# Softmax of three wide-head attentions: one exp for each head and sequence, with the maximum as its bias and the sum as its second result

## The chip, the cores and the metric

The kernel runs on one core of a Trainium2 chip. Its time is device microseconds of one execution; the figure compared is the median of several runs. A separate execution was recorded by the hardware profiler, and all durations of single instructions come from that one. The core's engines are TensorE (PE in the profile; its weight loads are PEld), VectorE (DVE), ScalarE (ACT), GpSimd (POOL) and SyncE (SP), which issues most DMAs. Each engine runs its own instructions in the order in which they were written, and waits on semaphores for the others.

## What is computed

The reference is a decoder of four layers on 32 sequences of 64 tokens of width 256, all in float32. Each layer adds an attention (or a state-space mixer), a cross attention to a context of 64 tokens of width 128, and a feed-forward part. The three attentions of the change are the wide ones:

- **L0_attn**: 32 heads of 64, 8 heads of keys and values, rotary positions, causal: `softmax((q k^T) / sqrt(64))`.
- **L0_xattn**: 16 heads of 128, a mask over the context; where a sequence's mask is empty the output is 0: `softmax(masked(q k^T) / sqrt(128))`.
- **L1_xattn**: 16 heads of 128 with q and k normalised by their root mean square: `softmax((q_n k_n^T) / sqrt(128))`.

```python
scores = jnp.einsum('bhqd,bhkd->bhqk', q, k) / jnp.sqrt(jnp.float32(HD))
scores = jnp.where(causal[None, None], scores, jnp.finfo(scores.dtype).min)
probs = jax.nn.softmax(scores, axis=-1)
o = jnp.einsum('bhqk,bhkd->bhqd', probs, v)
```

## The kernel before

The 2048 tokens are 16 tiles of 128 tokens, so a tile is two whole sequences. Every tile's residual stays on the chip (`X[i]`). The tiles run in three groups of 8, 6 and 2. A group runs its wide stages (L0_attn, L0_xattn, L0_ffn, L1_attn, L1_xattn) while the group before it runs the later, narrow ones, the two streams interleaved by `weave`. The first group runs its first stages alone: L0_attn and L0_xattn of 8 tiles, then L0_ffn and L1_attn, then L1_xattn. A tile has four wide softmaxes: two in L0_attn (16 heads each; `unit_L0_attn`'s loop over `u`), one in L0_xattn and one in L1_xattn. That makes 64 in all.

One softmax works on a tile `s` of 128 partitions x 16 x 64: for each query on its partition, 16 groups of 64 scores, which is one head of one sequence each. TensorE writes the scores to PSUM, and VectorE moves them to `s`, adding the mask or multiplying by the normaliser. Then come five steps on `s`: `shift` takes the maximum of each group (VectorE) and subtracts it from the 1024 columns (`combine`: VectorE or GpSimd); ScalarE takes the exp of all 1024 columns in one instruction, with the attention's scale; `weigh` adds up each group and takes the reciprocal (VectorE); another `combine` multiplies. L0_xattn multiplies the 16 reciprocals by `some`, which is 0 for an empty mask. Then `turn` transposes `s` on TensorE, eight blocks of 128x128, and the products with the values and the output weights follow (`cross_out` in the cross attentions).

Nothing is issued in the order of this code. A `Recorder` collects every operation with the tiles that it reads and writes, and `Order` writes down one fixed order for each engine: it keeps a clock for each engine, prices each operation with `duration`, and again and again takes the operation that can start first, the oldest one where several can. Work may be taken up to 120 us of TensorE work ahead of the oldest open operation, as long as buffers are free: 8 PSUM banks (`mm`), 10 wide tiles (`b4`), 35 small ones (`sm`) and others. An operation of `either` or `combine` may go to two engines, and the planner picks the one that ends it earlier by its prices. In the profile every instruction has line 2340, where the planned order is issued; the instructions are told apart by the names of their tiles, which come from the function that asked for them (`shift_sm`, `weigh_sm`, `L_xattn_b`, `turn_mm`). The prices that the prediction uses are these:

```python
        if method.startswith("reduce") and views[1].dims[-1][0] > 1:
            return 0.15 + n * 0.0017
        return 0.15 + n * 0.00104 + 0.06 * small
    if engine == "scalar":
        if method == "activation":
            return (0.17 if psum else 0.205) + n * 0.00083 + 0.18 * (small and psum)
...
    return 0.14 + n * (0.00174 if full < 2 else 0.0022)
EARLY = {"vector": 0.082, "scalar": 0.1, "gpsimd": 0.04}
```

Here `n` is the number of columns, the last return is GpSimd's, and `EARLY` is how long before the end of an operation the engine takes its next one in the plan.

Of the kernel before, what the change touches and what calls it, by code (L numbers as in the profile page):

```python
# [21 lines left out]
AF = mybir.ActivationFunctionType  # L22
# [18 lines left out]
def _constants():  # L41

    f = np.float32
    r = np.arange(P)
    c = {}
    c["ident"] = np.eye(P, dtype=f)
    c["ones"] = np.ones((P, P), f)

    c["causal"] = np.where(np.arange(64)[None, :] <= (r % 64)[:, None], 0.0, NEG).astype(f)

    c["upto"] = ((r % 64)[:, None] <= np.arange(64)[None, :]).astype(f)

    c["after"] = ((r[:, None] > r[None, :]) & (r[:, None] // 64 == r[None, :] // 64)).astype(f)

    c["before"] = (r[:, None] < r[None, :]).astype(f)

    c["strip8"] = ((r[:, None] % 32) // 8 == np.arange(4)[None, :]).astype(f)
    c["strip16"] = ((r[:, None] % 32) // 16 == np.arange(2)[None, :]).astype(f)

    c["parity"] = (r[:, None] // 64 == np.arange(2)[None, :]).astype(f)  # L60

    c["unit"] = np.broadcast_to(np.eye(1, 32, dtype=f), (P, 32))
    c["iota"] = np.broadcast_to(np.arange(64, dtype=f), (P, 64))
    main = ((r % 64) < 48).astype(f)
    c["mainT"] = np.zeros((P, P), f)
    c["mainT"][0], c["mainT"][1] = main, 1 - main
    c["row"] = r[:, None].astype(f)

    at = (np.arange(NT)[:, None, None] * P + r[None, :, None]) * 6 + np.arange(6)[None, None, :] - NONE
    c["parts"] = np.transpose(at, (1, 0, 2)).reshape(P, NT * 6).astype(f)  # L70
    c["mhalf"] = np.full((P, 32), -0.5, f)

    inv = f(1.0) / f(500000.0) ** (np.arange(0, 64, 2, dtype=f) / f(64))
    ang = inv[r % 32][:, None] * np.arange(64, dtype=f)[None, :]
    co, si = np.cos(ang).astype(f), np.sin(ang).astype(f)
    c["rope0"] = np.concatenate([co, si, si, co], 1)
    inv = f(1.0) / f(10000.0) ** (np.arange(0, 8, 2, dtype=f) / f(8))
    ang = (r % 64).astype(f)[:, None] * inv[None, :]
    co, si = np.cos(ang).astype(f), np.sin(ang).astype(f)
    c["rope3"] = np.concatenate([co, co, -si, si], 1)  # L80
    at, parts, n = {}, [], 0
    for k, v in c.items():
        at[k] = (n, n + v.shape[1])
        n += v.shape[1]
        parts.append(v.astype(f))
    return np.ascontiguousarray(np.concatenate(parts, 1)), at
# [113 lines left out]
def bc(ap, axis, n):  # L200

    u = ap.unsqueeze(axis)
    s = list(u.shape)
    s[axis] = n
    return u.broadcast_to(s)
# [11 lines left out]
def split(ap, a, pat="p (a b) -> p a b"):  # L217
    return ap.rearrange(pat, a=a)
# [157 lines left out]
class Recorder:  # L376
# [7 lines left out]
    def add(self, ways, args, kw, group=None):  # L384

        op = Op()
        op.at, op.ways, op.args, op.kw, op.group, op.behind = len(self.ops), ways, args, kw, group, []
        out = kw["out"] if "out" in kw else args[0]
        op.outs = [out] if isinstance(out, (View, Far)) else []
        views = [v.view if isinstance(v, Rows) else v for v in [*args, *kw.values()]]  # L390
        op.ins = [v for v in views if isinstance(v, (View, Far)) and v is not out]
        op.after, op.tiles, before = [], set(), {}
        for views, write in ((op.ins, False), (op.outs, True)):
            for v in views:
                t, m = v.t, v.mask()
                lo, hi = v.p0, v.p0 + v.n
                if t.psum:
                    lo, hi = 0, P
                op.tiles.add(t)
                for kept in (t.writes, t.reads) if write else (t.writes,):  # L400
                    covered = False
                    for o, l2, h2, m2 in kept:
                        if o is not op and m & m2 and lo < h2 and l2 < hi and (group is None or o.group != group):
                            before[o.at] = True
                            covered = covered or (write and not (m2 & ~m) and lo <= l2 and h2 <= hi)
                    if covered:
                        same = lambda a: group is not None and a[0].group == group
                        kept[:] = [a for a in kept if a[3] & ~m or a[1] < lo or a[2] > hi or same(a)]
        for views, write in ((op.ins, False), (op.outs, True)):
            for v in views:  # L410
                lo, hi = (0, P) if v.t.psum else (v.p0, v.p0 + v.n)
                (v.t.writes if write else v.t.reads).append((op, lo, hi, v.mask()))
        op.waits, op.ready = len(before), 0.0
        for i in before:
            self.ops[i].after.append(op)
            if self.ops[i].group is not None:
                op.behind.append(self.ops[i])
        for t in op.tiles:
            t.left += 1
            if t.first is None:  # L420
                t.first = op.at
            t.last = op.at
        self.ops.append(op)
# [234 lines left out]
class Net:  # L658
# [163 lines left out]
            self.nc.vector.scalar_tensor_tensor(x, ps, rs, x, ALU.mult, ALU.add)  # L822


    def weigh(self, s, sums_of):

        n = s.shape[1]
        sm, r = self.sm(n), self.sm(n)
        self.nc.vector.reduce_sum(sm, sums_of, AX.X)
        self.nc.vector.reciprocal(r, sm)  # L830
        return r

    def shift(self, out, s):

        n, m = s.shape[1], s.shape[2]
        mx = self.sm(n)
        self.nc.vector.reduce_max(mx, s, AX.X)
        self.nc.combine(out, s, bc(mx, 2, m), ALU.subtract)

    def turn(self, p, n):  # L840

# [24 lines left out]
    def unit_L0_attn(self, layer, W, i):  # L866
# [53 lines left out]
        for u in range(2):  # L920

            s = self.b4(16, 64)
            for j in range(2):
                nc.vector.tensor_tensor(
                    s[:, 8 * j : 8 * j + 8], split(sc[2 * u + j], 8), bc(self.k("causal"), 1, 8), ALU.add
                )
            self.shift(s, s)
            nc.scalar.activation(s, s, AF.Exp, scale=0.125)
            r = self.weigh(s, s)
            nc.combine(s, s, bc(r, 2, 64), ALU.mult)  # L930
            ss.append(s)
        terms = []
        for u in range(2):
# [118 lines left out]
    def unit_L0_xattn(self, layer, W, i):  # L1052
        nc = self.nc
        wq, wo = W
        hT = self.norm(layer, [i])
        cx, cT, mu = self.context(i), self.contextT(i), self.tile("cx", P, dtype=U8)
        nc.sync.dma_start(out=mu, in_=self.ins["mask"][i * P : (i + 1) * P].partition_broadcast(P))

        qs = []
        for a in range(2):  # L1060
            q = self.b4(8, P)
            for j in range(0, 8, 4):
                ps = split(self.mm(), 4)
                for u in range(4):
                    self.prod(ps[:, u, :], [(wq[a][:, j + u, c * P : (c + 1) * P], hT[:, c, :]) for c in range(2)])
                self.evac(q[:, j : j + 4, :], ps)
            qs.append(q)
        mf, add, some = self.tmp(P), self.tmp(P), self.sm(2)
        nc.vector.tensor_copy(mf, mu)
        nc.vector.tensor_scalar(add, mf, 1.0, -NEG, ALU.subtract, ALU.mult)  # L1070
        nc.vector.reduce_max(some, split(mf, 2), AX.X)
        ps = self.cross_scores(qs, lambda h, b: cT[:, b * 64 : b * 64 + 64])
        s = self.b4(16, 64)
        for j in range(2):
            nc.vector.tensor_tensor(
                s[:, 8 * j : 8 * j + 8].rearrange("p (a b) n -> p a (b n)", b=2), split(ps[j], 4), bc(add, 1, 4), ALU.add
            )
        self.shift(s, s)
        nc.scalar.activation(s, s, AF.Exp, scale=128.0**-0.5)
        r = self.weigh(s, s)  # L1080

        nc.vector.tensor_tensor(split(r, 8), split(r, 8), bc(some, 1, 8), ALU.mult)
        nc.combine(s, s, bc(r, 2, 64), ALU.mult)
        self.cross_out(i, s, cx, wo, "x0_")


# [278 lines left out]
    def unit_L1_xattn(self, layer, W, i):  # L1365
# [58 lines left out]
        for b in range(4):  # L1424
            self.transpose(pt[:, b, :], rows[:, b * P : (b + 1) * P])
        ve, rq = self.sm(4, 2, 2), self.sm(4, 2, 2)
        nc.vector.tensor_scalar(
            ve, pt.rearrange("p (a b) (m r) -> p m a b r", a=2, r=32)[:, :, :, :, 0], 1.0 / 128, 1e-5, ALU.mult, ALU.add
        )
        self.power(rq.rearrange("p a b c -> p (a b c)"), ve.rearrange("p a b c -> p (a b c)"))  # L1430
        ps = self.cross_scores(qs, lambda h, b: kTs[h // 8][:, h % 8, b * 64 : b * 64 + 64])
# [2 lines left out]
        for j in range(2):  # L1434
            at = slice(8 * j, 8 * j + 8)
            nc.vector.tensor_tensor(s[:, at], split(ps[j], 8), bc(rq[:, at], 2, 64), ALU.mult)
        self.shift(s, s)
        nc.scalar.activation(s, s, AF.Exp, scale=128.0**-0.5)
        r = self.weigh(s, s)
        nc.combine(s, s, bc(r, 2, 64), ALU.mult)  # L1440
        self.cross_out(i, s, cx, wo, "x1_")


# [995 lines left out]
```

## Time and profile before

| | |
|---|---|
| median of 3 runs | 3205.41 us (3201.11 to 3210.14) |
| the profiled execution | 3220.28 us, its span 3218.4 us |
| mean granted TensorE clock | 0.963 |
| wide softmaxes | 64 (32 in L0_attn, 16 in L0_xattn, 16 in L1_xattn) |

The span runs from the first to the last instruction of the profiled execution. A row of a group of instructions reads: line, engine, operation, output tile and its inputs without buffer numbers, shapes, count, then busy time and mean nanoseconds of one, then the engine's idle time just before them and what ended it. In a row of waits the numbers are the total in microseconds, how many times, and the longest. A timeline row starts with its start and its length in microseconds.

### The profile page before, as it was taken

Reading aid. Unit: us, or ns where it says so; the run is one execution under the profiler, and the core shown is the slowest. Engines: PE = TensorE matmul, PEld = TensorE weight load, DVE = VectorE, ACT = ScalarE, POOL = GpSimd, SP = SyncE. Lnnn points to the kernel's source line nnn. Section 1 sums busy time; section 2 is a strip of 40 time slices with the busy share of each in tenths; the row PEclk is TensorE's granted clock in tenths of the full one; section 3 lists DMA queues with packets and bytes.
Section 4 is the critical chain, followed back from the end, with each engine's and each line's share of the span. In section 5 each row is a group of like instructions: output and inputs, shape, how many; then the busy total and the mean of one; then the engine's idle time right before and its main releaser. Section 6 shows DMA issues by size and latency. Waiting matters only on the chain.

```text
span 3218.4 us, 66418 instructions
## 1 busy us (share of the span) xinstructions
PE 3007.1 (93%) x26862; PEld 2378.3 (74%) x26862; DVE 2124.8 (66%) x5250; ACT 1421.4 (44%) x2643; POOL 1373.5 (43%) x1240
## 2 busy tenths in 40 slices
PE   8999999999999999999999999999999989997689
PEld 6888887777777877787777677677777767775466
DVE  5673347675456667655879986676656787776673
ACT  1233325656442333433555655554335554444341
POOL 4442142214464555225653455454634664443420
PEclk9999999999999899999989999898999999997899
DMA  4103320031431433111000010022562120222450
GB/s 153 33 28 133 110 70 1 18 126 57 177 129 49 153 124 103 50 44 61 27 32 23 2 65 21 25 83 90 177 218 76 38 89 15 69 97 88 141 189 14
DMA packets 112950, 256.99 MB, mean 80 GB/s; under 512 B 26309, under 2 KB 73688, under 8 KB 100228
## 3 DMA queue, kind: packets, MB, share of 16 engines
q1 hardware_dynamic: 97860, 204.73, 18.1%
q0 software_dynamic: 14784, 48.01, 4.4%
q8 instruction: 213, 3.49, 0.4%
q14 instruction: 93, 0.76, 0.1%
HBM read 177.34 MB, written 78.77 MB: 80 GB/s over the span
## 4 chain that ended last, share of the span: by engine, by line
PE 63%; DVE 23%; ACT 5%; POOL 4%; issue 3%; DMA 1%; SPq 0%; POOLq 0%; DVEq 0%; ACTq 0%
PE L_xattn_mm L2340 8%; PE cross_out_mm L2340 8%; PE ssm_heads_mm L2340 8%; PE L_attn_mm L2340 7%; PE pair_mm L2340 5%; DVE ssm_heads_b L2340 4%; PE L_ffn_mm L2340 4%; PE turn_mm L2340 3%; PE L_block_mm L2340 3%; PE rope_mm L2340 3%; DVE L_xattn_b L2340 2%; PE L_dense_mm L2340 2%; DVE L_attn_b L2340 2%; PE L_experts_mm L2340 2%; DVE L_xattn_sm L2340 2%
## 5 line engine op out<-in xcount | busy, mean ns | idle before, releaser
L2340 PE MATMUL pair_mm<-norm_b,load_ssm_w 128*128 128x256 f32 x1280 | 306.4, 384 | 0.3 <-DVE heads_b L2340 0.3
L2340 PEld LDWEIGHTS pair_mm<-norm_b,load_ssm_w 128*128 128x128 f32 x1280 | 236.6, 191 | 44.0 <-issue 8.2
L2340 POOL TENSOR_TENSOR norm_sm<-norm_sm,__init___consts 128x1 f32<-128x1 f32 (+1 forms) x142 | 88.1, 624 | 341.6 <-DVE norm_sm L2340 333.2
L2340 POOL TENSOR_TENSOR L_xattn_sm<-L_xattn_sm,__init___consts 128x8 f32<-128x8 f32 (+2 forms) x62 | 178.2, 2879 | 85.8 <-DVE L_xattn_sm L2340 62.0
L2340 ACT COPY turn_b<-turn_mm 128x512 f32<-128x512 f32 x237 | 130.8, 589 | 171.5 <-PE turn_mm L2340 167.5
L2340 DVE SCALAR_TENSOR_TENSOR ssm_heads_b<-pair_mm,load_ssm_wp,ssm_heads_b 128x252 f32<-128x252 f32 (+2 forms) x480 | 193.6, 465 | 11.8 <-ACT ssm_heads_b L2340 11.4
L2340 ACT ACT_TABLE_LOAD x146 | 187.3, 1283 | 10.1 <-PE ssm_heads_mm L2340 3.4
L2340 ACT COPY L_xattn_b<-L_xattn_mm 128x512 f32<-128x512 f32 x180 | 105.9, 589 | 179.9 <-PE L_xattn_mm L2340 179.3
L2340 PE MATMUL rope_mm<-norm_b,load_L_attn_w 128*128 128x128 f32 x1280 | 169.4, 289 | 5.1 <-DMA load_L_attn_w<-in_a_wk 4.8
L2340 PEld LDWEIGHTS rope_mm<-norm_b,load_L_attn_w 128*128 128x128 f32 x1280 | 159.6, 202 | 10.9 <-issue 9.2
L2340 PE MATMUL ssm_heads_mm<-load_ssm_w,ssm_heads_b 128*128 128x256 f32 x640 | 158.2, 390 | 7.1 <-POOL ssm_heads_b L2340 7.0
L2340 PEld LDWEIGHTS ssm_heads_mm<-load_ssm_w,ssm_heads_b 128*128 128x128 f32 x640 | 115.6, 190 | 44.3 <-issue 16.0
L2340 DVE TENSOR_TENSOR __init___x<-__init___x,cross_out_mm 128x256 f32<-128x256 f32 x32 | 13.4, 420 | 200.2 <-PE cross_out_mm L2340 200.2
L2340 POOL TENSOR_TENSOR ssm_heads_b<-ssm_heads_b,ssm_heads_b 128x1024 f32<-128x1024 f32 x28 | 66.9, 2388 | 183.1 <-DVE ssm_heads_b L2340 171.2
L2340 ACT COPY norm_b<-norm_mm 128x256 f32<-128x256 f32 (+1 forms) x132 | 54.9, 438 | 170.3 <-PE norm_mm L2340 166.3
L2340 PEld LDWEIGHTS L_xattn_mm<-norm_b,load_L_xattn_w 128*128 128x128 f32 x1024 | 122.3, 194 | 10.0 <-issue 7.7
L2340 PE MATMUL L_xattn_mm<-norm_b,load_L_xattn_w 128*128 128x128 f32 x1024 | 128.7, 280 | 0.8 <-DVE __init___x L2340 0.8
L2340 POOL TENSOR_TENSOR L_attn_b<-rope_b 128x256 f32<-128x256 f32 x132 | 99.4, 768 | 67.0 <-DVE rope_b L2340 53.5
L2340 DVE TENSOR_SCALAR norm_b<-__init___x,norm_sm,norm_sm 128x256 f32<-128x256 f32 x192 | 93.6, 505 | 48.2 <-POOL norm_sm L2340 39.6
L2340 PEld LDWEIGHTS cross_out_mm<-load_L_xattn_w,cross_out_b 128*128 128x128 f32 x512 | 99.7, 197 | 32.9 <-ACT cross_out_b L2340 17.2
L2340 PE MATMUL cross_out_mm<-load_L_xattn_w,cross_out_b 128*128 128x256 f32 x512 | 120.0, 394 | 4.2 <-ACT cross_out_b L2340 3.3
L2340 PE MATMUL L_xattn_mm<-norm_b,units_L_xattn_w 128*128 128x128 f32 x1024 | 120.8, 277 | 2.0 <-DVE norm_sm L2340 1.2
(438 smaller groups left out, 7874.1 us busy)
## 6 DMA issues: line engine op xcount, KB each, us to landing
queue<-far_w SPq DMA_DIRECT2D x14, 1024.0 KB, 17.0
L_block_w<-in_f_rows SPq DMA_DIRECT2D x16, 770.0 KB, 4.4
load_ssm_w<-in_s_in SPq DMA_DIRECT2D x12, 1024.0 KB, 5.3
parts<-far_w SPq DMA_DIRECT2D x10, 1024.0 KB, 16.3
slots<-far_w SPq DMA_DIRECT2D x16, 548.0 KB, 6.7
L_experts_b<-slots SPq DMA_DIRECT2D x32, 274.0 KB, 4.2
units_L_xattn_w<-kept_x SPq DMA_DIRECT2D x8, 1024.0 KB, 10.3
L_parts_b<-parts SPq DMA_DIRECT2D x14, 512.0 KB
```

What stands on the lines that cost most here:

```text
L2340: done = getattr(getattr(nc, e), method)(*map(real, op.args), **{k: real(v) for k, v in op.kw.items()})
```

## The change

The subtraction of the maximum, the one wide exp and the sum are replaced by 16 exps of 64 columns, one for each head and sequence. Each takes the negated maximum of its group as its bias, a pointer to one column, and gives the sum of its results as a second output (`accum_out`) to one column of a small tile. The reciprocal and the final multiplication stay. In L0_attn the scale moves into the tables of the rotary positions, and in L1_xattn into the normaliser of the queries, so their exps have scale 1. In L0_xattn the exp keeps its scale, the negated maximum is scaled and capped at 1e28 and the sums are held at 0.5 or more, which replaces `some`. The recorder learns that an operation can have two outputs. The planner's prices are not touched.

```diff
-    co, si = np.cos(ang).astype(f), np.sin(ang).astype(f)
+    co, si = ((g(ang.astype(float)) * 0.125**0.5).astype(f) for g in (np.cos, np.sin))
     c["rope0"] = np.concatenate([co, si, si, co], 1)
...
-        op.outs = [out] if isinstance(out, (View, Far)) else []
+        op.outs = [v for v in (out, kw.get("accum_out")) if isinstance(v, (View, Far))]
...
-    def weigh(self, s, sums_of):
-        n = s.shape[1]
-        sm, r = self.sm(n), self.sm(n)
-        self.nc.vector.reduce_sum(sm, sums_of, AX.X)
-        self.nc.vector.reciprocal(r, sm)
-        return r
-    def shift(self, out, s):
-        n, m = s.shape[1], s.shape[2]
-        mx = self.sm(n)
-        self.nc.vector.reduce_max(mx, s, AX.X)
-        self.nc.combine(out, s, bc(mx, 2, m), ALU.subtract)
+    def exps(self, s, less, sums=None, scale=1.0):
+        for j in range(s.shape[1]):
+            at = slice(j, j + 1)
+            kw = {} if sums is None else {"accum_out": sums[:, at]}
+            self.nc.scalar.activation(s[:, j], s[:, j], AF.Exp, bias=less[:, at], scale=scale, **kw)
+    def softmax(self, s, scale=1.0, cap=None):
+        nc, n, m = self.nc, s.shape[1], s.shape[2]
+        mx, sums, r = self.sm(n), self.sm(n), self.sm(n)
+        nc.vector.reduce_max(mx, s, AX.X, negate=True)
+        if cap is not None:
+            nc.vector.tensor_scalar(mx, mx, scale, cap, ALU.mult, ALU.min)
+        self.exps(s, mx, sums, scale)
+        if cap is not None:
+            nc.vector.tensor_single_scalar(sums, sums, 0.5, ALU.max)
+        nc.vector.reciprocal(r, sums)
+        nc.combine(s, s, bc(r, 2, m), ALU.mult)
...
@@ unit_L0_attn
-            self.shift(s, s)
-            nc.scalar.activation(s, s, AF.Exp, scale=0.125)
-            r = self.weigh(s, s)
-            nc.combine(s, s, bc(r, 2, 64), ALU.mult)
+            self.softmax(s)
...
@@ unit_L0_xattn
-        nc.vector.reduce_max(some, split(mf, 2), AX.X)
...
-        self.shift(s, s)
-        nc.scalar.activation(s, s, AF.Exp, scale=128.0**-0.5)
-        r = self.weigh(s, s)
-        nc.vector.tensor_tensor(split(r, 8), split(r, 8), bc(some, 1, 8), ALU.mult)
-        nc.combine(s, s, bc(r, 2, 64), ALU.mult)
+        self.softmax(s, 128.0**-0.5, 1.0e28)
...
@@ unit_L1_xattn
-            ve, pt.rearrange("p (a b) (m r) -> p m a b r", a=2, r=32)[:, :, :, :, 0], 1.0 / 128, 1e-5, ALU.mult, ALU.add
+            ve, pt.rearrange("p (a b) (m r) -> p m a b r", a=2, r=32)[:, :, :, :, 0], 1.0, 128e-5, ALU.mult, ALU.add
...
-        self.shift(s, s)
-        nc.scalar.activation(s, s, AF.Exp, scale=128.0**-0.5)
-        r = self.weigh(s, s)
-        nc.combine(s, s, bc(r, 2, 64), ALU.mult)
+        self.softmax(s)
```

More of the change, by code (lines that the diff above doesn't have):

```diff
@@ L388, in add @@
         out = kw["out"] if "out" in kw else args[0]
-        op.outs = [out] if isinstance(out, (View, Far)) else []
+        op.outs = [v for v in (out, kw.get("accum_out")) if isinstance(v, (View, Far))]
         views = [v.view if isinstance(v, Rows) else v for v in [*args, *kw.values()]]
-        op.ins = [v for v in views if isinstance(v, (View, Far)) and v is not out]
+        op.ins = [v for v in views if isinstance(v, (View, Far)) and not any(v is o for o in op.outs)]
         op.after, op.tiles, before = [], set(), {}
@@ L1067, in unit_L0_xattn @@
             qs.append(q)
-        mf, add, some = self.tmp(P), self.tmp(P), self.sm(2)
+        mf, add = self.tmp(P), self.tmp(P)
         nc.vector.tensor_copy(mf, mu)
         nc.vector.tensor_scalar(add, mf, 1.0, -NEG, ALU.subtract, ALU.mult)
-        nc.vector.reduce_max(some, split(mf, 2), AX.X)
         ps = self.cross_scores(qs, lambda h, b: cT[:, b * 64 : b * 64 + 64])
```

## The prediction

> **What bounds the kernel now.** I read the page first, for who is busy.
>
> ```profile
> PE 3007.1 (93%) x26862; PEld 2378.3 (74%) x26862; DVE 2124.8 (66%) x5250; ACT 1421.4 (44%) x2643; POOL 1373.5 (43%) x1240
> PEclk9999999999999899999989999898999999997899
> PE 63%; DVE 23%; ACT 5%; POOL 4%; issue 3%; DMA 1%; SPq 0%; POOLq 0%; DVEq 0%; ACTq 0%
> ```
>
> TensorE has work in 3007.1 of 3218.4 us. All its idle time is 211 us, so a faster softmax can gain only a part of that, while a slower one has no ceiling. ScalarE, to which the change moves work, is idle more than half the time. What counts is whether TensorE is made to wait. So second: the waits of TensorE, at the transpositions (`turn`) that follow the softmaxes.
>
> ```profile
> PE turn_mm L2340 <- DVE L_xattn_b L2340: 9.9, 5, 5.1
> PE turn_mm L2340 <- POOL L_xattn_b L2340: 9.8, 13, 2.8
> PE turn_mm L2340 <- DVE L_attn_b L2340: 2.4, 3, 1.6
> PE turn_mm L2340 <- POOL L_attn_b L2340: 2.1, 2, 1.5
> ```
>
> These 24.2 us are all that TensorE now loses directly to the 64 softmaxes. Third: the timeline around one of them, an L0_xattn tile while the group runs alone.
>
> ```profile
> 319.71 1.22 DVE L2340 TENSOR_REDUCE shift_sm<-L_xattn_b 128x16 f32<-128x1024 f32 x1
> 321.10 1.90 POOL L2340 TENSOR_TENSOR L_xattn_b<-L_xattn_b,shift_sm 128x1024 f32<-128x1024 f32 x1 [3.68 <-DVE shift_sm L2340]
> 323.04 1.06 ACT L2340 ACTIVATE L_xattn_b<-L_xattn_b 128x1024 f32<-128x1024 f32 x1 [0.61 <-POOL L_xattn_b L2340]
> 324.13 1.22 DVE L2340 TENSOR_REDUCE weigh_sm<-L_xattn_b 128x16 f32<-128x1024 f32 x1 [3.19 <-ACT L_xattn_b L2340]
> 325.38 0.25 DVE L2340 RECIPROCAL weigh_sm<-weigh_sm 128x16 f32<-128x16 f32 x1
> 325.99 1.90 POOL L2340 TENSOR_TENSOR L_xattn_b<-L_xattn_b,weigh_sm 128x1024 f32<-128x1024 f32 x1 [2.98 <-DVE weigh_sm L2340]
> 328.51 1.04 PE L2340 MATMUL turn_mm<-__init___consts,L_xattn_b 128*128 128x128 f32 x8
> ```
>
> From the start of the maximum to the end of the multiplication are 8.2 us (319.71 to 327.89), and the turn starts 0.6 us later. I put each of the 64 multiplications beside its turn in the timeline: the median distance is 0.15 us in the cross attentions and 0.7 us in L0_attn, and only eleven are over 2 us. So waits are short not because there is room but because the written order brings TensorE to the turn just as the result is ready. A chain that gets longer meets TensorE waiting.
>
> Fourth: what a wait costs beyond itself, by windows before, in and after the longest such wait (the fields after the busy times are the granted clock, the DMA share and GB/s).
>
> ```profile
> 2360.00:2383.40 23.40, 22.91 (x292) 21.82 (x290) 5.76 (x11) 8.54 (x14) 8.19 (x10) 1.00 0.83 300
> 2383.40:2388.50 5.10, 0.04 (x1) 0.04 (x1) 5.01 (x7) 1.79 (x4) 3.88 (x5) 1.00 0.64 239
> 2388.60:2392.00 3.40, 3.40 (x16) 1.87 (x19) 3.40 (x9) 1.17 (x2) 2.52 (x3) 0.50 0.37 111
> ```
>
> The clock is 1.00 before and in the 5.1 us wait, 0.50 for 3.4 us after it. Of the 20 TensorE gaps over 2 us behind the first 20 us, 18 go with such a stretch; the mean clock of 0.963 is 119 us lost to them.
>
> **The change, part by part.** Four rows price it.
>
> ```profile
> L2340 POOL TENSOR_TENSOR L_attn_b<-L_attn_b,shift_sm 128x1024 f32<-128x1024 f32 x30 | 57.0, 1904 | 95.3 <-DVE shift_sm L2340 90.0 <-PE L_route_mm L2340 5.1
> L2340 ACT ACTIVATE ssm_sm<-ssm_sm 128x64 f32<-128x64 f32 x16 | 4.1, 257 | 0.2
> L2340 ACT ACTIVATE L_dense_b<-L_dense_mm 128x256 f32<-128x256 f32 x16 | 6.1, 383 | 48.5 <-PE L_dense_mm L2340 48.5
> L2340 ACT ACTIVATE L_experts_b<-L_experts_mm,L_experts_sm 128x256 f32<-128x256 f32 x37 | 15.6, 471 | 17.7 <-PE L_experts_mm L2340 17.5
> ```
>
> *Removed.* 64 subtractions (59 on GpSimd at 1.90 us, 5 on VectorE), 64 wide exps (1.06 us) and 64 sums (1.21 us): 112 us of GpSimd, 68 of ScalarE, some 85 of VectorE. L0_xattn also loses a 0.28 us maximum and a 0.17 us multiplication a tile and gains two vector instructions on 16 columns, at the same 0.17 us: nothing in sum. The negated maximum, the constants of the rotation and the 128 folded into L1_xattn's power cost nothing: the same instructions with other numbers.
>
> *Added.* 64 x 16 = 1024 exps of 128x64 with a pointer as bias, each with a sum. 128x64 without pointer takes 257 ns. A pointer adds 471 - 383 = 88 ns, and back-to-back copies of 585 ns in the timeline follow each other every 0.48 us, so 0.1 us overlaps: about 0.25 us an exp before the sum. No row shows a sum written out by ScalarE. From below it is free, 0.25 in all; cheaper than that it can't be, as each exp still passes its 64 columns. From above it is a second instruction with a pointer and no overlap: the shortest activation (128x1) takes 0.19 us, with a pointer 0.28, and the exp's own overlap goes too: 0.35 + 0.28 = 0.63. I take 0.44, the exp and one shortest instruction without a pointer, which is the nearest row. A softmax then holds ScalarE 16 x 0.44 = 7.0 us in place of 1.06, in all 450 us for 68 (44% busy becomes some 53%).
>
> [...]
>
> *The path.* New chain: maximum 1.21, hand-over 0.15, exps 16p, hand-over and reciprocal 0.35, hand-over 0.15, multiplication 1.90: 3.8 + 16p (L0_xattn 0.3 more). With p = 0.44 a cross softmax takes 10.8 to 11.1 us against 8.2 to 8.4. In L0_attn two softmaxes of a tile start 2.3 us apart. Before, the second overlaps the first on three engines and ends 11.6 us after the first maximum (67.03 to 78.62 in the timeline); now its exps queue behind the first's, 3.8 + 32p = 17.9 us, 6.3 late. Put against each softmax's own turn in the old order, counting a pair once, the lateness sums to 54 us over the 16 L0_attn tiles and 34 over the 32 cross tiles: **+88**. By the same count: 0 at p = 0.25, 31 at 0.35, 164 at 0.54, 238 at 0.63.
>
> *The order.* It is written by the planner with its own prices: an exp of 64 columns is 0.258 us less 0.1, so 16 are 2.6 us in its plan; it drops 1.9 + 1.06 + 1.9 for what is removed. Its chain gets 2.2 us shorter, while the chip's gets longer, and it takes the oldest ready work first: turns move up to 2.2 us forward on TensorE. 48 places x 2.2 = 106 at most; some have distance in hand: **+65**. Behind the exps in ScalarE's queue stand the copies that empty PSUM for TensorE's other work; they are late by the same time, inside the same wait, so I add nothing.
>
> *The clock.* At p = 0.44 some 30 of 48 waits are over 2 us. The 25 half-clock stretches now are 9.7 us on average, so each costs 4.8 us: 144 if all of them trigger one. Many will be cut up by small pieces of work: **+65**. [...]
>
> *Relief.* Up to 24 us of the waits shown, and VectorE, 23% of the chain, has 85 us less to do, though little of it where its slices are fullest (1600 to 1850 us, where L1_attn runs): **-40**, between 0 and -80.
>
> Sum: 3220.3 (the profiled execution) + 88 + 65 + 65 - 40 = 3398. The median of the runs is 15 us under the profiled one, so I predict **3380**.
>
> **The rivals.** *Faster:* the sum costs nothing and p is about 0.25. Then 3.8 + 4.0 is 7.8 us against 8.2 to 9, even the pairs end at 11.8, the order's shift eats little, and relief stands: -40 to -80, **3125 to 3165**. For: ScalarE is 56% idle and its exps overlap. It decides below p = 0.27 ((8.2 - 3.8) / 16). Against: 16 sums must each reach their own column. Chance 0.17. *Twice as slow:* no overlap, p = 0.63: 238 + 80 + 120 - 40 = **+400, 3605**. Chance 0.13. *Hidden:* p about 0.3, lateness of some 15 + 40 less 40, that is **3195 to 3250**: the woven groups, where TensorE has other streams' work, cover the rest. For: eleven turns already have over 2 us in hand. Chance 0.18, of which 0.06 falls within 0.3% (about 10 us, what this kernel's runs can tell from no change) and 0.01 below. My forecast, **3270 to 3480**, has 0.52.
>
> **How the numbers follow.** Faster 0.18, same 0.06, slower 0.76. The range reaches from the middle of the gap to the faster case, 3170, to p = 0.54 with its clock loss (164 + 75 + 110 - 40 = +309, 3515): 3170 to 3520 leaves out about 0.1 on either side.
>
> **What would show it.** A row of 1024 exps of 128x64, its pitch near 0.44 us, with or without a row of its own for the sum; ScalarE near 1800 us; no subtraction and no sum on GpSimd and VectorE; waits of TensorE at the turns grown from 24 to 150 us or more, over half of it in the first 420 us; more half-clock stretches, most of them in the first 1000 us, where there is none now. I am wrong if the pitch is under 0.3 us, or if it is 0.44 and the waits at the turns stay under 60 us.

## The result, and the profile after

The median of four runs is **3381.0 us** (3377.6 to 3381.7) against 3203.4 for four runs of the kernel before (3201.1 to 3210.1): a ratio of **1.0552, 95% interval 1.0537 to 1.0566**. The change makes the kernel 5.5% slower. The profiled execution took 3377.6 us, with a span of 3375.6 us and a mean granted clock of 0.943.

From the page after come the busy times, the clock in 40 slices, and the shares of the chain that ended last.

```profile
PE 3053.1 (90%) x26862; PEld 2406.2 (71%) x26862; DVE 2031.1 (60%) x5235; ACT 1684.9 (50%) x4591; POOL 1260.5 (37%) x1173
PEclk9989999999999989999998999899999999988689
PE 57%; DVE 18%; ACT 15%; POOL 4%; issue 3%; DMA 2%; SPq 0%; POOLq 0%; ACTq 0%; DVEq 0%
```

VectorE and GpSimd lost 94 and 113 us of work, ScalarE gained 264, and ScalarE's share of the chain went from 5% to 15%. Yet no engine became the bound: ScalarE is busy half the time. TensorE has the same 26862 matmuls, and they take 46 us more (3053.1 for 3007.1); its idle time, span less busy time, went from 211 to 322 us. 46 + 111 is the whole growth of the span, 157 us. The 46 us go with the clock: the stretches in which the granted clock is 0.50 grew from 25 with 239.3 us in all to 56 with 387.7 us. Half of the 148 us more, 74 us, is what the clock took, partly from time in which TensorE had nothing to do.

TensorE's waits at the transpositions that follow the softmaxes (total, times, longest) were 24.2 us before:

```profile
PE turn_mm L2336 <- POOL L_xattn_b L2336: 59.1, 23, 7.9
PE turn_mm L2336 <- DVE L_xattn_b L2336: 14.7, 6, 5.8
PE turn_mm L2336 <- DVE L_attn_b L2336: 12.0, 5, 2.8
PE turn_mm L2336 <- POOL L_attn_b L2336: 8.4, 6, 1.8
```

These are 94.2 us now, most of them in the cross attentions, where a turn waits for the multiplication. A second wait is new. Before the change there was none of it, now it has 20.9 us in 13 times:

```profile
PE L_attn_mm L2336 <- ACT turn_b L2336: 20.9, 13, 2.5
```

Here the turn itself is done, and TensorE waits for the copies that ScalarE makes of its result. Eight of the 13 waits, 13.8 us, lie in the first group's L0_attn. In six of these, and in nine of all, the copies come on ScalarE straight behind the exps of another softmax. Some rows around one such place show it; the turn ends at 144.90 us, and the first copy starts 1.7 us later, when the last exp is over.

```profile
143.81 1.09 PE L2336 MATMUL turn_mm<-__init___consts,L_attn_b 128*128 128x128 f32 x8 [1.80 <-POOL L_attn_b L2336]
146.30 0.33 ACT L2336 ACTIVATE L_attn_b<-L_attn_b,softmax_sm 128x64 f32<-128x64 f32 x1
146.63 1.04 ACT L2336 COPY turn_b<-turn_mm 128x512 f32<-128x512 f32 x2
147.24 1.13 PE L2336 MATMUL L_attn_mm<-turn_b,L_attn_b 64*64 64x256 f32 x8 [1.48 <-ACT turn_b L2336]
```

The waits at the turns grew by 70 us and this one by 21, together 91 of the 111 us of idle time that came in. What an exp and its sum cost is in ScalarE's groups of instructions (busy time, mean ns, idle time before them and who ended it):

```profile
L2336 ACT ACTIVATE L_attn_b<-L_attn_b,softmax_sm 128x64 f32<-128x64 f32 x512 | 169.9, 334 | 60.5 <-DVE softmax_sm L2336 60.4
L2336 ACT ACTIVATION_READ_ACCUMULATOR L_attn_b<-L_attn_b,softmax_sm 128x1 f32 x512 | 96.0, 187 | 0.0
L2336 ACT ACTIVATE L_xattn_b<-L_xattn_b,softmax_sm 128x64 f32<-128x64 f32 x512 | 170.2, 334 | 13.1 <-DVE softmax_sm L2336 10.3 <-DVE L_route_sm L2336 2.7
L2336 ACT ACTIVATION_READ_ACCUMULATOR L_xattn_b<-L_xattn_b,softmax_sm 128x1 f32 x512 | 96.1, 188 | 0.0
```

The sum is an instruction of its own in the records, 188 ns behind each exp of 334 ns. The timeline around one L0_xattn softmax, the counterpart of the one shown in the prediction, says how the two overlap (rows of other engines' work and of two short steps on VectorE are left out).

```profile
381.67 1.21 DVE L2336 TENSOR_REDUCE softmax_sm<-L_xattn_b 128x16 f32<-128x1024 f32 x1
383.19 0.35 ACT L2336 ACTIVATE L_xattn_b<-L_xattn_b,softmax_sm 128x64 f32<-128x64 f32 x1 [1.36 <-DVE softmax_sm L2336]
383.44 0.19 ACT L2336 ACTIVATION_READ_ACCUMULATOR L_xattn_b<-L_xattn_b,softmax_sm 128x1 f32 x1
383.54 0.33 ACT L2336 ACTIVATE L_xattn_b<-L_xattn_b,softmax_sm 128x64 f32<-128x64 f32 x1
...
388.41 0.19 ACT L2336 ACTIVATION_READ_ACCUMULATOR L_xattn_b<-L_xattn_b,softmax_sm 128x1 f32 x1
388.84 0.25 DVE L2336 RECIPROCAL softmax_sm<-softmax_sm 128x16 f32<-128x16 f32 x1
389.27 1.90 POOL L2336 TENSOR_TENSOR L_xattn_b<-L_xattn_b,softmax_sm 128x1024 f32<-128x1024 f32 x1 [22.52 <-DVE softmax_sm L2336]
391.22 1.09 PE L2336 MATMUL turn_mm<-__init___consts,L_xattn_b 128*128 128x128 f32 x8 [2.58 <-POOL L_xattn_b L2336]
```

The read starts 0.25 us after its exp, while the exp is still running, and the next exp starts 0.10 us after that. Sixteen pairs take 5.4 us, 0.34 us each (over all softmaxes, the median from one exp to the next is 0.331). From the start of the maximum to the end of the multiplication are now 9.5 us, 1.3 more than before. The turn starts 0.05 us after the multiplication's end and TensorE has been idle for 2.58 us: twice what the chain grew. The same wait stands at all eight L0_xattn turns of the first group (2.6 to 2.9 us each).

Last, the windows of the first group's L0_attn and L0_xattn, before and after (length; busy time of PE, PEld, DVE, ACT, POOL; granted clock, DMA share, GB/s). A stage ends here with the last addition to the residual of its last tile. Before:

```profile
0.00:256.00 256.00, 238.35 (x2446) 197.86 (x2447) 158.73 (x263) 65.57 (x116) 106.48 (x113) 1.00 0.19 72
256.00:422.00 166.00, 161.63 (x1500) 137.51 (x1499) 54.45 (x107) 54.54 (x97) 35.29 (x22) 1.00 0.33 122
```

After:

```profile
0.00:293.00 293.00, 249.87 (x2431) 206.74 (x2432) 136.26 (x250) 126.97 (x596) 79.21 (x97) 0.93 0.16 59
293.00:502.00 209.00, 185.77 (x1554) 152.79 (x1553) 51.12 (x114) 89.96 (x350) 22.98 (x16) 0.93 0.28 103
```

The two stages take 80 us more, half of all that the span lost. TensorE's idle time in them went from 22.0 to 66.4 us (+44), and its work from 400.0 to 435.6 us (+36) as the clock fell from 1.00 to 0.93. In L0_xattn eight waits, 21.7 us in sum, stand beside 24 us more of matmul time. Some 6 of these are the 54 matmuls more in this window, and some 14 the clock: seven half-clock stretches with 27 us in all, half of it lost. So a wait of 2.7 us costs about two thirds as much again behind it. ScalarE is busy for 43% of these windows: it isn't full here either.

### The profile page after: what moved, and what is told of

It reads as the page before. It is cut to its first block, busy times and chain, and to the rows that moved or that the text cites. A ratio compares the mean times of both kernels' runs of the same rounds, so it can differ in the third digit from the quotient of the medians.

```text
span 3375.6 us, 68213 instructions
## 1 busy us (share of the span) xinstructions
PE 3053.1 (90%) x26862; PEld 2406.2 (71%) x26862; DVE 2031.1 (60%) x5235; ACT 1684.9 (50%) x4591; POOL 1260.5 (37%) x1173
## 4 chain that ended last, share of the span: by engine, by line
PE 57%; DVE 18%; ACT 15%; POOL 4%; issue 3%; DMA 2%; SPq 0%; POOLq 0%; ACTq 0%; DVEq 0%
PE cross_out_mm L2336 8%; PE ssm_heads_mm L2336 7%; PE L_xattn_mm L2336 7%; PE L_attn_mm L2336 7%; ACT L_xattn_b L2336 6%; PE pair_mm L2336 5%; ACT L_attn_b L2336 5%; DVE ssm_heads_b L2336 4%; PE L_ffn_mm L2336 3%; PE turn_mm L2336 3%; PE L_block_mm L2336 2%; PE rope_mm L2336 2%; PE L_dense_mm L2336 2%; PE L_experts_mm L2336 2%; DVE L_xattn_b L2336 2%
## 5 line engine op out<-in xcount | busy, mean ns | idle before, releaser
L2336 DVE SCALAR_TENSOR_TENSOR ssm_heads_b<-pair_mm,load_ssm_wp,ssm_heads_b 128x248 f32<-128x248 f32 (+2 forms) x480 | 193.3, 465 | 12.5 <-ACT ssm_heads_b L2336 12.2
L2336 ACT ACTIVATE L_attn_b<-L_attn_b,softmax_sm 128x64 f32<-128x64 f32 x512 | 169.9, 334 | 60.5 <-DVE softmax_sm L2336 60.4
L2336 ACT ACTIVATE L_xattn_b<-L_xattn_b,softmax_sm 128x64 f32<-128x64 f32 x512 | 170.2, 334 | 13.1 <-DVE softmax_sm L2336 10.3
L2336 ACT COPY L_xattn_b<-L_xattn_mm 128x512 f32<-128x512 f32 x160 | 92.4, 587 | 156.2 <-PE L_xattn_mm L2336 156.0
L2336 POOL TENSOR_TENSOR L_attn_b<-rope_b 128x256 f32<-128x256 f32 x113 | 82.2, 740 | 160.8 <-DVE rope_b L2336 158.5
L2336 PE MATMUL turn_mm<-__init___consts,L_xattn_b 128*128 128x128 f32 x384 | 66.2, 324 | 82.9 <-POOL L_xattn_b L2336 59.1
L2336 POOL TENSOR_TENSOR L_xattn_b<-L_xattn_b,softmax_sm 128x1024 f32<-128x1024 f32 x26 | 51.5, 1981 | 219.2 <-DVE softmax_sm L2336 182.8
L2336 DVE TENSOR_TENSOR rope_b<-rope_mm,__init___consts 128x512 f32<-128x512 f32 x160 | 105.4, 680 | 46.1 <-PE rope_mm L2336 27.4
```

The source lines that it names most:

```text
L2336: done = getattr(getattr(nc, e), method)(*map(real, op.args), **{k: real(v) for k, v in op.kw.items()})
```

## The experiments

The theory (A): TensorE's order is the plan's, and the plan has the softmax *shorter* while the chip has it longer. Its chain lost 1.92 + 1.06 + 1.21 = 4.2 us and gained 16 x 0.158 + 0.1 = 2.6, so it is 1.6 us shorter; the chip's is 1.3 us longer. The turn is placed some 2.9 us too early, TensorE stands there, and half-clock matmuls follow. The rival (B): the chip's longer chain, or ScalarE's load, costs the time whatever the plan says. The kernels below ran on several chips, which the record numbers. On chip 14 the kernel before takes 3204 us, as it did beside the result; on chips 4, 15 and 3 it takes 3325, 3324 and 3329 us. So each kernel is compared with the kernel before on its own chip, as a ratio. Where two such ratios from different chips are set against each other, a difference between the chips can be in it.

**Prices alone, the exps untouched.** The kernel before, with one wide exp, and with the planner's price of the maximum and of the sum lowered from 1.21 to 0.15 us. Its instructions on the chip are the same; only the order can change.

```diff
     if engine == "vector":
+        if out.t.name.startswith(("shift", "weigh")) and method.startswith("reduce"):
+            return 0.15
```

> The kernel before with the planner's price of the maximum and of the sum of the wide softmaxes lowered from 1.2 to 0.15 us each; the instructions on the chip are those of before. The plan of a softmax is then 2.1 us too short, as it is 2.4 us too short in the changed kernel. Theory A: TensorE waits some 2.5 us at most cross-attention turns, the clock falls after them, and the time rises to between 3280 and 3370 us, with no exp on the chip changed. Theory B: nothing that ScalarE does is different, so the time stays within 3195 to 3230 us.

Measured, on chip 14: 3312.9 us, ratio **1.0325** (1.0283 to 1.0367), in A's range and far outside B's. TensorE's waits at the turns:

```profile
PE turn_mm L2342 <- POOL L_xattn_b L2342: 27.1, 18, 2.4
PE turn_mm L2342 <- POOL L_attn_b L2342: 23.0, 9, 3.6
PE turn_mm L2342 <- DVE L_xattn_b L2342: 23.0, 8, 6.7
PE turn_mm L2342 <- DVE L_attn_b L2342: 5.7, 5, 1.8
```

78.8 us for 24.2, with 41 half-clock stretches (323 us), and TensorE idle for 282 us. The first two stages end at 485 us, nearer to the change (502) than to the kernel before (422). A plan that is 2.1 us too short for each softmax does all that by itself, for 104 us, without one of the new exps.

**The true price.** The change, with 0.175 us more in the plan for an exp with a sum: 0.333 in all, what the chip takes.

```diff
-            return (0.17 if psum else 0.205) + n * 0.00083 + 0.18 * (small and psum)
+            return (0.17 if psum else 0.205) + n * 0.00083 + 0.18 * (small and psum) + 0.175 * ("accum_out" in kw)
```

> The changed kernel with one number of the planner changed: an exp that gives its sum is priced 0.175 us dearer, so that 16 of them take 5.3 us in the plan, as on the chip, and not 2.5. Theory A (the plan): the loss is TensorE brought to the turns too early by its own plan; with the true price its waits at the turns fall from 94 us to under 40, the half-clock stretches go, and the time falls to between 3210 and 3270 us. Theory B (ScalarE): 32 exps in a row hold ScalarE for 10.7 us, the chain of an L0_attn pair is 3 us longer than before whatever the order, and the time stays above 3330 us.

Measured, on chip 4: ratio 1.0265 (1.0241 to 1.0289). The waits at the turns, and the windows of the first two stages:

```profile
PE turn_mm L2336 <- POOL L_xattn_b L2336: 10.9, 11, 4.0
PE turn_mm L2336 <- DVE L_xattn_b L2336: 6.5, 4, 3.4
PE turn_mm L2336 <- POOL L_attn_b L2336: 1.1, 1, 1.1
PE turn_mm L2336 <- DVE L_attn_b L2336: 0.5, 1, 0.5
```

```profile
0.00:269.00 269.00, 254.64 (x2451) 209.52 (x2452) 147.62 (x273) 119.55 (x579) 80.43 (x102) 0.97 0.19 68
269.00:435.00 166.00, 161.78 (x1509) 138.96 (x1508) 58.19 (x123) 78.33 (x325) 21.16 (x15) 1.00 0.33 123
```

The waits at the turns are 19.0 us, less than before the change, those for ScalarE's copies in L0_attn fell from 20.9 to 1.1 us, and L0_xattn takes 166 us at a clock of 1.00, as it did before, with 16 exps to each softmax. The longer chain costs nothing there once the plan knows it. But the total is 2.7% up, above A's range (1.002 to 1.021 as ratios) and below B's (over 1.039): A names what the waits come from, and something else remains. The change itself and two other prices, all three on chip 15:

> The changed kernel as it is, on the same chip as the two runs beside it: 1.045 to 1.065 times the kernel before if the loss does not hang on the chip.

Measured: 1.053 (1.0503 to 1.0557). The loss isn't one chip's; its waits at the turns are 90.1 us here.

> The changed kernel with the exp that gives its sum priced 0.18 us dearer in place of 0.175: the same program with another order, to see how much of the 2.65% that the true price left is the accident of one order. Theory A: the order is all of the loss; another order with the same truth lands anywhere from 1.000 to 1.03 times the kernel before. Theory C: about half of the loss is the order and half stays with 450 us of exps and sums in ScalarE's queue; between 1.015 and 1.035.

Measured, with 0.18 in place of 0.175: 1.0187 (1.0167 to 1.0207). Between this and 1.0265 lie 0.005 us in a price, and so another order, and another chip: the ratio moved by 0.008.

> The same with 0.25 us, so that 16 exps take 6.5 us in the plan and 5.3 on the chip: ScalarE is planned too full. Theory A: being early costs, being late in the plan costs little; 1.00 to 1.03. Theory C: 1.02 to 1.04. A ratio of 1.05 or more would say that the price itself, not its truth, is what moves the time.

Measured, with 0.25: 1.0201 (1.0178 to 1.0224). More distance than the chip needs buys nothing. This value and 1.0187 lie where the ranges of A and C overlap, so they don't decide between the two. The true price thus takes the ratio from 1.053 to between 1.019 and 1.027: 0.026 to 0.034 of the loss is the price's, half to two thirds, some 85 to 110 us of 3204.

**Is the rest the first group's?** The exps stay in the eight tiles of the first group; later groups go back to a subtraction, one wide exp and a sum on VectorE (an empty mask is not handled there). One kernel has the true price (0.18), one the old.

```diff
         nc.vector.reduce_max(mx, s, AX.X, negate=True)
+        if self.tile_now >= GROUPS[0]:
+            nc.combine(s, s, bc(mx, 2, m), ALU.add)
+            nc.scalar.activation(s, s, AF.Exp, scale=scale)
+            nc.vector.reduce_sum(sums, s, AX.X)
+            nc.vector.reciprocal(r, sums)
+            nc.combine(s, s, bc(r, 2, m), ALU.mult)
+            return
```

> Exps with sums at the true price (0.18 us dearer), but only for the 8 tiles of the first group; the tiles of the later groups, whose softmaxes run beside other streams, keep subtraction, one wide exp and the sum on VectorE (an empty mask is not handled there). With the true price the first group ended its L1_xattn at 1004 to 1013 us against 1001, and all the rest of the loss came later, most of it in the L1_xattn of the second group. Theory C1: the exps of the later groups cost it; here the ratio is 1.000 to 1.008. Theory C2: it is the accident of the order in the later groups, which any change of the order draws anew; 1.003 to 1.025.

> The same with the planner's price of the change. The changed kernel was 87 us late when the first group ended its L1_xattn (1089 against 1002 us), 37 at L0_attn, 43 at L0_xattn, and with the true price 3 to 12. So here that point is reached 80 to 95 us late, and the ratio is the one of the run beside it plus 0.024 (0.020 to 0.029).

Measured, on chip 3: 1.0094 (1.0067 to 1.0122) with the true price, 1.0306 (1.0279 to 1.0333) with the old. The first group's wide stages end at 1003 and 1087 us. So the wrong price costs 0.021 in the first group alone, where no other stream has work to fill the wait: some 60 to 80% of all it costs. With the true price and the exps in the first group only, 0.009 is left, above C1's range and in C2's. Another 0.009 to 0.017 comes when later groups have them, by ratios from different chips.

**The sums on VectorE.** Exps as in the change but without the second result; VectorE adds up, as before.

```diff
-        self.exps(s, mx, sums, scale)
+        self.exps(s, mx, None, scale)
+        nc.vector.reduce_sum(sums, s, AX.X)
```

> The changed kernel with the 16 exps without their sums; VectorE adds up the groups as before (1.21 us). The planner's prices are those of the change. An exp then takes about 0.24 us, 3.9 us for 16, and the chain 1.2 + 0.15 + 3.9 + 1.3 + 0.4 + 1.9 = 8.9 us, against 7.5 in the plan. Theory A: what counts is chip minus plan, 1.4 us here, 2.9 in the changed kernel and 0.4 in the kernel before, so about 40% of the loss: 3250 to 3310 us. Theory B: ScalarE is held 7.8 us for a pair in place of 10.7, about two thirds of the loss: 3300 to 3340 us.

Measured, on chip 14: 3281.7 us, ratio 1.0231 (1.0194 to 1.0269), within A's range and below B's; waits at the turns 48.3 us. An exp without a sum is followed by the next at 0.24 us (in the kernel measured next, 512 of L0_attn's take 124.4 us), so the plan is only 16 x (0.24 - 0.16) = 1.3 us short for each softmax, and the loss is less than half. Then the same with that gap priced (0.08 us more for each such exp):

> 16 exps without sums, VectorE adds up the groups, and the exps are priced 0.08 us dearer, as the chip shows them (0.24 us each). Theory A: chip and plan agree as in the kernel before (0.1 to 0.4 us apart), so the loss of 77 us with the old price goes but for 0 to 30 us: 3200 to 3235 us. Theory B: ScalarE's 7.8 us for a pair remain: 3260 to 3290 us.

Measured, on chip 4: 1.018 (1.0158 to 1.0202). A had expected about 1.00 to 1.01: a miss, and 1.018 lies in B's range (1.017 to 1.027). But it doesn't come where B puts it: in the profile the second group's L1_attn ends at 1922 us, as in the kernel before at the high price (below, same chip), with 50 of the 64 softmaxes done; what it loses against that kernel comes later. Here too some 2% remains, and ScalarE reads no sum here, so the remainder isn't the price of the reads.

**A shorter chain.** One maximum for a query's 16 groups, one wide exp with it as a pointer bias, sums on VectorE (a softmax only as long as a group's scores lie near their query's maximum). It drops the subtraction, 2 us of the chain, and adds nothing.

```diff
-        nc.vector.reduce_max(mx, s, AX.X, negate=True)
+        nc.vector.reduce_max(mx, s.rearrange("p a b -> p (a b)"), AX.X, negate=True)
...
-        self.exps(s, mx, sums, scale)
+        nc.scalar.activation(s, s, AF.Exp, bias=mx, scale=scale)
+        nc.vector.reduce_sum(sums, s, AX.X)
```

> One maximum for each query over all its 16 groups in place of 16, one exp of 1024 columns with it as a pointer bias, sums on VectorE. The softmax is the same as long as a group's scores lie near the query's maximum. The chain is 1.2 + 0.15 + 1.15 + 0.05 + 1.2 + 0.4 + 1.9 = 6.1 us, against 8.2 before, 64 subtractions are gone from GpSimd, and ScalarE has 64 exps as before. Theory A: chip and plan (5.8 us) agree, so the waits at the turns stay small, and a shorter chain gains little behind a TensorE that is 93% busy: 3160 to 3215 us. Theory B: ScalarE as before, subtraction gone: the same range or a little less, 3140 to 3200 us.

Measured, on chip 14: 3217.3 us, ratio 1.0058 (1.0037 to 1.008), where a gain was expected. Its page:

```profile
PE 2995.0 (93%) x26862; PEld 2371.6 (74%) x26862; DVE 2087.7 (65%) x5245; ACT 1426.0 (44%) x2644; POOL 1253.1 (39%) x1182
```

120 us less of GpSimd, 37 of VectorE, 12 of TensorE, and no gain. The first group's wide stages end 8 us earlier than before (994 for 1002) and the last wide stage 46 us earlier (2743 for 2789); the last, narrow part takes 463 us for 429 and gives it back. In this kernel a softmax that is shorter than the old one, in the plan and on the chip, is worth nothing at the end.

**More distance at the turns.** If turns that come early cost time, later ones might gain: the kernel before with 1.6 us as the price of the maximum and of the sum, and the one-maximum kernel with the same.

> The kernel before with the planner's price of the maximum and of the sum of the wide softmaxes raised from 1.2 to 1.6 us each, 0.8 us in all; the instructions are those of before. In the kernel before the chip is 0.4 us over its plan, so the plan is now longer than the chip. Theory A: the waits at the turns of the 64 softmaxes, 24 us, go, and the time falls by 10 to 40 us: 3165 to 3195 us. Theory B: the order of the kernel before costs nothing; 3195 to 3215 us.

> One maximum for each query and one wide exp (as in the run before it), with the same two prices raised to 1.6 us. The run with one maximum was not faster than the kernel before although its chain is 2 us shorter. If its plan still brought TensorE too early somewhere, this gives 3165 to 3200 us. If the softmax is off the path altogether once it is on time, and only the accident of the order remains, it stays within 1% of the kernel before on either side: 3180 to 3230 us.

Measured, on chip 4: 1.0035 (1.002 to 1.0049) and 1.004 (1.0021 to 1.0058). No gain; the expectation of 10 to 40 us missed. Three kernels with no small exps in them, all in another order and two with less work besides, stand at 1.004 to 1.006: that much a new order seems to cost by itself here. No version beat the kernel before.

**Where the rest is.** By the ends of stages, with the kernel before at the high price (1.0035) for comparison. The columns are from chips 4, 15, 3 and 15, on which the kernel before takes the same time to 0.2%:

| end of | before, high price | true price (0.18) | first group only, true price | the change |
|---|---|---|---|---|
| first group's L0_xattn | 422 | 430 | 429 | 501 |
| first group's L1_xattn | 1001 | 1004 | 1003 | 1088 |
| second group's L1_attn | 1922 | 1935 | 1916 | 2031 |
| second group's L1_xattn | 2284 | 2351 | 2306 | 2428 |
| span | 3347 | 3377 | 3357 | 3498 |

Up to 1922 us the true price takes back 96 of the 109 us by which the change is late. What it does not take back arises in one stage, the second group's L1_xattn, 416 us for 362. Its windows, the kernel before at the high price first, then the true price:

```profile
1922.00:2284.00 362.00, 335.36 (x3134) 246.80 (x3133) 243.82 (x579) 188.52 (x373) 189.38 (x154) 0.94 0.12 41
```

```profile
1935.00:2351.00 416.00, 352.55 (x3218) 260.35 (x3217) 251.15 (x623) 212.51 (x550) 186.85 (x155) 0.91 0.12 40
```

TensorE's work is 17 us longer, partly for the 84 matmuls more that fall into it, and its idle time 37 us (63.5 for 26.6), with ScalarE about half busy. Small exps aren't needed for most of that. The kernel with one maximum at the high price has none at all, and the one with exps in the first group only has none in this stage; on chips 4 and 3 they take 397 and 390 us for it, with TensorE busy for 351 and 353 us and idle for 46 and 37. The first of the two:

```profile
1897.00:2294.00 397.00, 350.88 (x3202) 261.42 (x3200) 248.79 (x607) 195.63 (x380) 174.38 (x148) 0.91 0.12 42
```

In the result's profiles the same stage took 359 us before and 360 after the change, and on chip 14 it took 362 us with 16 exps and the sums on VectorE. On chips 4, 15 and 3 it took 362 to 436 us, and 397 after the change, with the *same* program. So the rest comes from this stage on those chips, some 30 of the 54 us with no small exp in it, and part of it from bursts described at the end. Whether the true price would leave as much on chip 14 was not measured, and what makes the stage longer still with small exps (416 to 436 us) stays open.

## Why the prediction came out right

3381 lies on the forecast of 3380, but to the microsecond that is luck: terms of the sum were off and made up for each other.

- **Mechanism: right.** "the written order brings TensorE to the turn just as the result is ready. A chain that gets longer meets TensorE waiting." The price experiment shows it apart from all else (1.0325 with no exp changed), and the true price removes it (L0_xattn back at 166 us). What counts is thus the chip's chain less the plan's; the prediction's two terms for lateness and order are two parts of it, which these runs don't price one by one.
- **The pitch: wrong.** 0.44 us was forecast, about 0.335 measured: the sum has a row of its own, but it overlaps its exp and the next exp starts before it ends. By the prediction's own count the lateness is then about 26 us (0 at 0.25, 31 at 0.35), not 88. ScalarE is at 1685 us, not 1800.
- **The order: right, its price read wrongly.** The plan's chain got 1.6 us shorter, not 2.2: `1.9` for the sum was the price of a strided reduction, these are contiguous at 1.21. The error of the plan is thus 1.6 + 1.3 = 2.9 us for each softmax, where the prediction had 2.2 + 2.6 = 4.8 for a cross one.
- **Cost of that error.** Lateness, order and clock were 88 + 65 + 65 = 218 us together for those 4.8 us, 45 for each microsecond. Measured: 104 us for 2.1 (prices alone), 85 to 110 for 2.9 (true price): 29 to 50 for each. The rate was about right. The error was three fifths of what was put, and its cost half.
- **The copies behind the exps: put at nothing.** "they are late by the same time, inside the same wait, so I add nothing." In L0_attn they come after the turn, and TensorE waits for them a second time: 20.9 us in 13 waits, none before. With the true price 1.1 us are left, so this too is part of the price of the order.
- **The clock, in what it costs.** The mean clock's loss, half the time at half clock, went from 120 to 194 us: +74 for a forecast of 65. The L0_xattn stage, with no idle gap of TensorE above 2.9 us, ran at 0.93. The profiles before and after show when: each stretch starts on a grid of 3.41 us, and most (18 of 24 before, 44 of 55 after) follow a slot of the grid in which TensorE was idle for 1.7 us or more, half of the slot (the last part has the numbers). Of the eight L0_xattn waits after the change, 2.6 to 2.9 us each, seven put 1.96 us or more of idle time into one slot and go with a half-clock stretch; the eighth, split into 1.79 and 0.80 us, goes with none. So here a wait cost the clock or not by where it fell, which the sum didn't have.
- **Relief: didn't come.** -40 was taken off for VectorE's and GpSimd's lighter load. The waits at the turns grew to 94 us instead, and the one-maximum kernel, with GpSimd lighter by 120 us and the chain 2 us shorter, gained nothing (1.0058). 0 was the end of that range to take.
- **What the sum didn't have.** On chips 15 and 4, 1.9 to 2.7% remains with the true price, 60 to 85 us on 3204. No term stands for it. The overestimate of 108 to 133 us (218 less 85 to 110) is made up by the 40 us of relief that didn't come and by this. That sets ratios of other chips beside the result; for the chip of the result only the total of the change is known.
- **From the profiled run to the median: off.** 15 us were taken off and the rest rounded down to 3380, as the profiled execution before lay 15 us above the median; after, it lies 3.4 us below. Profile against profile the change is 157 us, 21 less than the 178 of the sum; median against median it is 178.
- **What would show it.** Right: 1024 exps with reads, no subtraction and no sum elsewhere, more half-clock stretches, and of the 148 us more 82 in the first 1000 us, where there was none. Wrong: the waits at the turns are 94 us, neither 150 nor under 60, and 26 of them, not over half, lie in the first 420 us. Yet half of the loss lies in the first 502 us, since slower matmuls follow the waits there (the clock went from 1.00 to 0.93).

The rivals: the faster case needed a pitch below 0.27, and even a pitch of 0.24, with the sums on VectorE, was slower (1.0231). The hidden case was near in its pitch of 0.3, and wrong in what follows: the first group has no other stream to cover a wait of 2.6 us.

## What to carry to other kernels

Where an order is written from a list of prices, an operation new to the list changes the order as well as the work; read the plan's price of it beside the measured one before the chip's own cost, since an error of 2 us at 64 places cost 100 us here with no instruction changed. In the first group's L0_xattn some 14 us lost to half-clock matmuls came with 21.7 us of TensorE's waits, so a wait counted about one and two thirds times there; and the first group, where one stream runs alone, had some 60 to 80% of what the wrong price cost. Taking work off engines that are not the bound gave nothing here (1.0058), even where the chain became shorter.

## What the runs showed of the hardware

- In the profile of the change each exp with a sum as second result has a second row on ScalarE, `ACTIVATION_READ_ACCUMULATOR`, 188 ns on average, 1024 in all. L0_attn's 512 exps of 128x64 with a pointer bias take 124.4 us without the sum (the sums on VectorE, the gap priced) and 169.9 us with it (the change), 0.24 and 0.33 us each, so the sum cost 0.1 us net.
- In the profiles before and after the change, the half-clock stretches of TensorE (25 and 56) start on one grid of 3.41 us, to within 0.01 us, and last 1 to 8 whole slots of it, 3.4 to 27.3 us (the last of each profile is cut short by the span's end). After the first 20 us, 20 slots before and 53 after had more than 2.0 us of TensorE idle in them, and each of them had a half-clock slot behind it; leaving out that last one, 18 of 24 stretches before and 44 of 55 after the change followed a slot with at least 1.7 us idle. The wait of 2.58 us shown above fell into two slots, 1.8 us into one, and has no stretch behind it.
- The change took 3381 us beside the result and 3500 on chip 15, the kernel before 3203 to 3204 there and on chip 14, and 3324 to 3329 on chips 4, 15 and 3: 3.5 to 4%. One place where it shows is the 84 indirect scatters of GpSimd (`slots`), which go in runs of 12 over some 15.5 us. In the result's profile of the change, other engines work on through such a run; in that of the true-price kernel on chip 4, they nearly stop (windows as above, the result's first):

```profile
2130.60:2147.20 16.60, 15.59 (x158) 11.44 (x156) 14.61 (x29) 12.57 (x30) 13.23 (x12) 1.00 0.29 102
```

```profile
2161.00:2176.20 15.20, 5.68 (x77) 3.57 (x75) 1.97 (x8) 0.00 (x0) 11.79 (x13) 0.73 0.30 103
```

In the seven runs of 12, TensorE was idle for 14 us in all before the change and 7 after it in the result's profiles; for 31 after the change on chip 15, with the same program; and on chips 4 and 15 for 27 us (before, high price) and 44 to 45 (true prices). Why the engines stop there was not found. Between the chips these are some 12 to 24 us of 120; the rest was not located.
